# Extra identity products on TensorE before real work in a fused convolution, attention and expert kernel

## Chip, cores and metric

The kernel runs on one core of a Trainium2 chip. The metric is device time in microseconds (us), taken as the median of several runs. A profiled execution gives the time of every instruction; all durations below come from it. TensorE is written PE in profile lines (its weight loads PEld), VectorE DVE, ScalarE ACT, GpSimd POOL, and the engine that issues most DMAs SP (its queue SPq).

## What is computed

The reference has two layers on an image batch x of shape 2 x 256 x 56 x 56, all in fp32. Layer 0 normalises x by groups of 8 channels, makes queries, keys and values by a 1x1 convolution and a depthwise 3x3 one, runs neighbourhood attention (7x7 windows, half the heads with dilation 2), projects, and adds x. Layer 1 works on the 6272 pixels as tokens: linear attention with a feed-forward block, then a mixture of 8 experts of which each token uses two. Cut to its last lines:

```python
# --- layer 0 (conv_attn_hybrid) ---
x = x + _L0_conv_ref(_gn(x), L0_conv_w_qkv1, L0_conv_w_qkv2, L0_conv_rpb0, L0_conv_rpb1, L0_conv_w_proj)
# --- layer 1 (conv_attn_hybrid) ---
t = _to_tokens(x)
t = t + _L1_attn_ref(_ln_t(t), ...)   # elu(q)+1, elu(k)+1, sums over keys, W1, relu, W2
t = t + _L1_ffn_ref(_ln_t(t), ...)    # top 2 of 8 experts: gelu(x W1 + b1) W2 + b2, weighted
x = _from_tokens(t, x)
```

## The kernel before, in words

**Stages in order of time.** (1) Layer 0 of the first image, up to some 420 us: statistics on VectorE, group sums by two tiny products (gps, L478 and L484), the 1x1 convolution (py, L521), the depthwise one (a few rows as products pc, L542, the rest on VectorE as yc, L564 and L571), then attention: scores s_ps (L644), exp on ScalarE, bias on VectorE (p, L649), values po (L658), and the projection (L344, L349). The second image's convolutions fill gaps from here on. (2) Layer 1's attention for the first half of the tokens (the first image). `keys` runs over pairs of token tiles of 128: it transposes them (pts, L278), multiplies by the key weights (kps, L297) and adds to the key sums (kx, L309). `prepare_feed_forward` makes a bias (hb, L1788) while keys run. `queries`, `message` (pm, L1905), `feed_forward` (p, L1935; py, L1951) and `route` then run over groups of four tiles, staggered. (3) From 750 to 1045 us, attention of the second image, with the end of the first half's routing and the first expert tiles among it. `prepare` transposes queries and keys of four rows in four parts (`part`, into tiles x, L759); `rest` allocates one po tile for a half band, adds two chunks of values into it, and `done` has VectorE add it to acc (L832). GpSimd scatters tokens to the experts' rows (L167, xs); SP reads them back as xr (L1536) together with the expert's weights w1e, w2e and b2e. (4) Layer 1's attention for the second half, with expert tiles in between. (5) Expert tiles alone: ph (L1600), gelu, py (L1618), scatter-add to y (L167). Before and after the last ones `write` reads y back as yr, transposes it (pto, L2337) and stores it.

**What sets the order.** Each engine runs its instructions in program order. In stages 2 to 5 the order on TensorE is written out by hand (`tc.manual_schedule`, with strings such as "mqfkpPPPP" that name which step comes next). On the other engines and the DMA queues a scheduler sets it from its own estimate of when each instruction becomes ready, so a change on TensorE can move instructions elsewhere. An instruction that waits holds up all behind it on its engine.

**PSUM tiles.** Each product writes a PSUM tile from a pool. A tile's first write waits until the readers of the tile that was there before are done. The attention of one image has one po tile (`bufs=1`, two banks); the pool of x has two tiles; pts, kps, hb, pm, pto come from small pools of one bank a tile. A matmul with `start=True` overwrites what is there.

A product of fp32 operands shows as two MATMUL records in the profile.

Of the kernel before, what the change touches and what calls it, by code (L numbers as in the profile page):

```python
# [20 lines left out]
P = 128  # L21
B, C, HH, WW = 2, 256, 56, 56
# [6 lines left out]
NA = -(-T // 128)  # L29
# [16 lines left out]
E = 8  # L46
# [79 lines left out]
def hybrid_kernel(ctx: ExitStack, tc: tile.TileContext, a: dict, out: bass.AP):  # L126
    nc = tc.nc
# [3 lines left out]
    ident = const.tile([P, P], F32, name="ident")  # L131
# [33 lines left out]
    def scatter(dst, index, src, mine, others, **kw):  # L165
# [5 lines left out]
        apart(ins.ins, mine, others)  # L171
        return ins.ins

    evac_n = [0]

    newest = [None, None, None]
# [89 lines left out]
    def keys(tk, wk, sm, ps, bank, w_k, b2, kx, acc, n0, n, p, first, last, eager):  # L266


        t = tk.at(n0, n)[p]
        rows = p.stop - p.start  # L270
        mv, rs = stats(sm, t, tk.up[p, n0 : n0 + n], p)
        xt = wk.tile([P, 2, C + E], F32, name="xt", tag="u", bufs=3)[p, :, :C]
        pts = ps.tile([P, 2, 2 * P], F32, name="pts", tag="a")
        for k in range(n):
            with tc.high_priority() if eager else nullcontext():
                norm(xt[:, k, :], t[:, k, :], mv, rs, k)
            for ct in range(2):
                nc.tensor.transpose(  # L278
                    pts[:, ct, k * P : k * P + rows], xt[:, k, ct * P : (ct + 1) * P], ident[p, p]
                )  # L280
        xT = tk.turned(n0, n)[:, :, p] if n == 1 else tk.turned(n0, n)
        with tc.high_priority() if eager else nullcontext():
            evac(xT, pts[:, :, : n * rows])

        up = sm.tile([P, 2, 2], F32, name="up")[p]
        nc.vector.tensor_scalar(up[:, 0, :n], rs[:, :n], 1.0, None, ALU.add)
        nc.vector.scalar_tensor_tensor(up[:, 1, :n], mv[:, :n, 0], -1.0, rs[:, :n], ALU.mult, ALU.mult)
        for k in range(n):
            nc.scalar.activation(
                t[:, k, :], t[:, k, :], AF.Identity, bias=up[:, 1, k : k + 1], scale=up[:, 0, k : k + 1]  # L290
            )
        nc.gpsimd.tensor_tensor(t, t, b2[p].unsqueeze(1).to_broadcast([rows, n, C]), ALU.add)
        yield
        kps = bank()[p]
        for k in range(n):
            for ct in range(2):
                nc.tensor.matmul(  # L297
                    kps[:, k, :], xT[:, ct, k * rows : (k + 1) * rows], w_k[:, ct, :],
                    start=(ct == 0), stop=(ct == 1),
                )  # L300
        ks = wk.tile([P, 2, C], F32, name="ks", tag="mn")[p]
        elu1(
            wk, ks[:, :n, :].rearrange("p k c -> p (k c)"), kps[:, :n, :].rearrange("p k c -> p (k c)"),
            "k", 4, p,
        )
        yield
        for k in range(n):
            for hg in range(2):
                nc.tensor.matmul(  # L309
                    kx[:, hg, :], ks[:, k, hg * P : (hg + 1) * P], xt[:, k, :],  # L310
                    start=(first and k == 0 and hg == 0), stop=(last and k == n - 1), skip_group_check=True,
                )
        if first:
            nc.gpsimd.tensor_copy(acc, ks)
        else:
            nc.gpsimd.tensor_tensor(acc[p, :n, :], acc[p, :n, :], ks[:, :n, :], ALU.add)
        yield
# [93 lines left out]
    class Convolutions:  # L411
# [49 lines left out]
        def norm_image(self):  # L461


            sp, x_sb = self.sp, self.x_sb
            st = sp.tile([P, 2, NG, 6], F32, name="st")
            mv = sp.tile([P, 2, 2], F32, name="mv")
            for gs in (range(0, 3), range(3, NG)):
                for ct in range(2):
                    for g in gs:
                        nc.vector.bn_stats(st[:, ct, g, :], x_sb[:, ct, g * G : (g + 1) * G])  # L470
            for ct in range(2):
                anchors["stats"] = nc.vector.bn_aggr(
                    mv[:, ct, :], st[:, ct, :, :].rearrange("p g s -> p (g s)")
                ).ins
            yield
            gps = self.bank([P, 4], "gps")
            gm = sp.tile([P, 2], F32, name="gm")
            nc.tensor.matmul(gps[:, 0:2], self.g8, mv[:, :, 0], start=True, stop=True)  # L478
            nc.vector.tensor_copy(gm, gps[:, 0:2])
            dv = sp.tile([P, 2], F32, name="dv")  # L480
            nc.vector.tensor_tensor(dv, mv[:, :, 0], gm, ALU.subtract)
            nc.vector.tensor_tensor(dv, dv, dv, ALU.mult)
            nc.vector.tensor_tensor(dv, dv, mv[:, :, 1], ALU.add)
            nc.tensor.matmul(gps[:, 2:4], self.g8, dv, start=True, stop=True)  # L484
            with tc.high_priority():
                grs, anchors["pow"] = rstd_of(sp, gps[:, 2:4], 1e-5, "gn")
            yield
            for c0, c1 in zip((0, G, T // 2), (G, T // 2, T)):
                cols = slice(c0, c1)
                for ct in range(2):  # L490
                    nc.vector.tensor_scalar(
                        x_sb[:, ct, cols], x_sb[:, ct, cols],
                        gm[:, ct : ct + 1], grs[:, ct : ct + 1], ALU.subtract, ALU.mult,
                    )

        def run(self):
# [6 lines left out]
            for b, oc in ((b, oc) for b in range(B) for oc in range(6)):  # L503
                diag = None
                for hf in range(2):
# [10 lines left out]
                    ypad = self.ypads[hf]  # L516
                    q0 = r0 - hf
                    for g0, n in ((0, 8), (8, 8), (16, 8), (24, 5)):
                        py = self.bank([P, 8, WW], "py")
                        for ct in range(2):  # L520
                            nc.tensor.matmul(  # L521
                                py[:, :n, :], self.wq1[:, ct, oc * P : (oc + 1) * P],
                                self.x_sb[:, ct, (q0 + g0) * WW : (q0 + g0 + n) * WW],
                                start=(ct == 0), stop=(ct == 1),
                            )
                        k0 = 1 - hf + g0
                        anchors["copied"] = nc.scalar.copy(  # L527
                            ypad[:, k0 : k0 + n, 1 : WW + 1], py[:, :n, :]
                        ).ins
                        if not shared:  # L530
                            yield b, oc
# [67 lines left out]
    class Attention:  # L599
# [116 lines left out]
        def run(self):  # L716
# [72 lines left out]
            def prepare(g):  # L789
# [15 lines left out]

                def part(k):
                    pm = banks()
                    turned(lds, k, pm)
                    settle(g, k, pm)

# [32 lines left out]
            def band0(r):  # L843
# [22 lines left out]
                def chunk(hf, c):  # L866
# [10 lines left out]
                    def rest():  # L877
                        if c == 2 * hf:
                            po = self.ps_o.tile([P, 2, 512], F32, name="po")
                            sums[0] = po[:, :, : ni * 31].rearrange("p k (i j) -> p k i j", j=31)  # L880
                        h0 = (0, 25)[hf]
                        sub = sums[0][:, :, :, j0 - h0 : j1 - h0]
                        self.values(
                            TT, got[0], [(None, q, 0, v0[:, c, :], sub[:, 0], sub[:, 1])], c == 2 * hf
                        )
# [461 lines left out]
    class Experts:  # L1347
# [106 lines left out]

        def full_tiles(self, pc, ones):

            ce = self.counts(self.wp, pc, ones, self.tk.cnt, "ce1")
            nt = self.steps_below(self.wp, ce, 1, ALU.is_ge, "full")
            yield
            self.tab_a = yield from self.table(self.wp, "A", NTA, nt, self.ebase)  # L1460
# [179 lines left out]
    def linear(ph, tk, half, behind=None):  # L1640
# [140 lines left out]
        def prepare_feed_forward():  # L1781
            with tc.issue_after(newest[0]):
                centre(fw2[:, :, :C])

            hb_ps = ps_h.tile([P, 512], F32, name="hb", tag="h")
            for oc in range(4):
                for k in range(2):
                    nc.tensor.matmul(  # L1788
                        hb_ps[:, oc : oc + 1], fw1[:, 2 + k, oc * P : (oc + 1) * P], g1b1[:, k, 1:2],
                        start=(k == 0), stop=(k == 1),  # L1790
                    )
# [103 lines left out]
        def message(n0, n, qz, out):  # L1895
# [2 lines left out]
            ss = sm.tile([P, 4], F32, name="ssm")  # L1898
            for k0 in range(0, n, 2):
                pm = ps_h.tile([P, 2, C], F32, name="pm", tag="h")  # L1900
                for k in range(min(2, n - k0)):
                    for b, c0, c1 in parts(n0, n):
                        p, at = (slice(c0, c1), 0) if n == 1 else (slice(0, P), (k0 + k) * P)
# [260 lines left out]
    def layer1(whole, tk, conv_ctx=None, conv=None, behind=None):  # L2164
# [14 lines left out]
        with ExitStack() as ph:  # L2179
# [30 lines left out]
            def ending():  # L2210
# [4 lines left out]
                    pass  # L2215
                next(todo)
                yield
                table = ex.full_tiles(ln.bank()[:, :E], ln.ones)
                next(table)
                next(todo)  # L2220
                yield
# [78 lines left out]
        with ExitStack() as ph:  # L2300
# [28 lines left out]
                    apart(ins.ins, [f"yread{run}"], [f"yend{run}"], "tokens of early groups")  # L2329
                return n0, n, yr  # L2330

            def write(n0, n, yr, engines, places):
                for ct in range(2):
                    pool, tag = places[ct]
                    pt = pool.tile([P, 512], F32, name="pto", tag=tag)
                    for k in range(n):
                        nc.tensor.transpose(  # L2337
                            pt[:, k * P : (k + 1) * P], yr[:, k, ct * P : (ct + 1) * P], ident
                        )
# [39 lines left out]
                for _ in ex.run([(t, 2) for t in range(NFS, NTL)] + [(k, 1) for k in range(NHS, E)], pools):  # L2379
                    pass  # L2380
            last = [read(n0, n, False) for n0, n in order[early2:]]
            for h in held + last:
                write(*h, (nc.scalar, nc.sync), [(ps_t, "pt"), (ps_h, "ph")])

    with ExitStack() as ph:
        tokens = Tokens(ph, 0)
# [48 lines left out]
```

## Time and profile before

| what | us |
|---|---|
| median of 3 runs | 2003.97 |
| lowest and highest run | 2000.4, 2013.45 |
| profiled execution, its own time | 2003.56 |
| span of the profiled execution, first to last instruction | 2001.8 |
| TensorE busy in the span | 1842.0 |
| VectorE, ScalarE, GpSimd busy | 1094.2, 704.5, 582.2 |

A line of the timeline gives start, duration, engine, source line, output and inputs, shape, how many records it stands for, and in brackets the idle time of the engine before it and what ended it. A line of a table of stretches gives the stretch, its length, each engine's busy time with instruction counts, the granted TensorE clock (1 is full speed), the share of time that the DMA engines are busy, and GB/s. A line of the waits gives total, times and longest.

### The profile page before, as it was taken

Reading aid. Unit: us, or ns where it says so; the run is one execution under the profiler, and the core shown is the slowest. Engines: PE = TensorE matmul, PEld = TensorE weight load, DVE = VectorE, ACT = ScalarE, POOL = GpSimd, SP = SyncE. Lnnn points to the kernel's source line nnn. Section 1 sums busy time; section 2 is a strip of 40 time slices with the busy share of each in tenths; the row PEclk is TensorE's granted clock in tenths of the full one; section 3 lists DMA queues with packets and bytes.
Section 4 is the critical chain, followed back from the end, with each engine's and each line's share of the span. In section 5 each row is a group of like instructions: output and inputs, shape, how many; then the busy total and the mean of one; then the engine's idle time right before and its main releaser. Section 6 shows DMA issues by size and latency. Waiting matters only on the chain.

```text
span 2001.8 us, 27731 instructions
## 1 busy us (share of the span) xinstructions
PE 1842.0 (92%) x9996; PEld 1308.3 (65%) x9996; DVE 1094.2 (55%) x2733; ACT 704.5 (35%) x1331; POOL 582.2 (29%) x634
## 2 busy tenths in 40 slices
PE   6999898988889996899989989999899999999996
PEld 3545354556555654566668756567688888888885
DVE  6978988888887746555557434554531212121221
ACT  2333324324434323445536433323322232323332
POOL 4630221025102444111126311445422222222221
PEclk9999999989999996999999999999999999999998
DMA  4753432340001534654474211114577676766995
GB/s 112 160 138 110 133 92 75 111 146 17 25 38 42 157 85 145 193 152 134 129 201 127 56 34 37 48 57 132 156 230 200 188 199 189 198 190 195 299 279 161
DMA packets 200153, 268.85 MB, mean 134 GB/s; under 512 B 30953, under 2 KB 158615, under 8 KB 199761
## 3 DMA queue, kind: packets, MB, share of 16 engines
q1 hardware_dynamic: 167920, 223.95, 37.0%
q0 software_dynamic: 19728, 27.54, 7.5%
q10 hardware_dynamic: 12352, 15.43, 2.2%
q8 instruction: 83, 1.36, 0.3%
q14 instruction: 70, 0.57, 0.1%
HBM read 200.19 MB, written 70.95 MB: 135 GB/s over the span
## 4 chain that ended last, share of the span: by engine, by line
PE 47%; DMA 4%; DVE 4%; ACT 3%; issue 1%; POOL 1%; SPq 0%; ACTq 0%; DVEq 0%; POOLq 0%
PE ph L1600 13%; PE py L1618 13%; PE p L1935 4%; PE x L1618 2%; DMA y<-yt,idi 2%; PE x L1600 2%; PE py L1951 2%; PE po L658 2%; DMA xr<-xs 1%; PE kx L309 1%; PE kp L297 1%; PE x L349 1%; PE pm L1905 1%; PE s_ps L644 1%; PE px L1569 1%
## 5 line engine op out<-in xcount | busy, mean ns | idle before, releaser
L1600 PE MATMUL ph<-xe,w1e 128*128 128x256 f32 (+1 forms) x1448 | 312.1, 371 | 15.3 <-ACT hT L1604 9.4
L1618 PE MATMUL py<-w2e,hT 128*128 128x256 f32 x1392 | 311.5, 379 | 0.0
L1604 ACT ACTIVATE hT<-ph,sv 128x256 f32<-128x256 f32 (+1 forms) x362 | 165.7, 462 | 393.4 <-PE ph L1600 386.1
L1600 PEld LDWEIGHTS ph<-xe,w1e 128*128 128x128 f32 x1448 | 262.6, 191 | 55.0 <-ACT hT L1604 11.2
L1618 PEld LDWEIGHTS py<-w2e,hT 128*128 128x128 f32 x1392 | 260.2, 190 | 33.2 <-issue 0.2
L167 POOL DMA_INDIRECT y<-yt,idi x101 | 160.2, 1587 | 325.4 <-DVE yt L1624 186.9
L571 DVE SCALAR_TENSOR_TENSOR yc<-ypad,w,yc 128x1120 f32<-128x1120 f32 x144 | 202.8, 1412 | 26.4 <-ACT yc L561 18.5
L261 POOL TENSOR_TENSOR rs<-rs,mhalf 128x2 f32<-128x2 f32 (+3 forms) x90 | 72.1, 805 | 323.6 <-DVE rs L260 292.7
L521 PE MATMUL py<-x_sb,wq 128*128 128x448 f32 (+1 forms) x384 | 153.8, 532 | 5.4 <-ACT ypad L527 3.8
L648 ACT ACTIVATE p<-s_ps 112x952 f32<-112x952 f32 (+5 forms) x88 | 102.1, 1160 | 154.6 <-PE s_ps L644 96.0
L1552 DVE CAST idi<-xr 128x2 int32<-128x2 f32 (+1 forms) x53 | 9.8, 184 | 258.6 <-DMA xr<-xs 258.4
L649 DVE TENSOR_TENSOR p<-p,tab 112x952 f32<-112x952 f32 (+5 forms) x88 | 122.0, 1389 | 45.5 <-ACT p L648 39.6
L542 PE MATMUL pc<-ypad,diag 128*128 128x448 f32 x324 | 131.9, 548 | 0.0
L1624 DVE SCALAR_TENSOR_TENSOR yt<-py,eq,yt 128x256 f32<-128x256 f32 x87 | 41.8, 482 | 156.6 <-PE py L1618 156.4
L1582 POOL TENSOR_SCALAR yt<-b2e,eq 128x256 f32<-128x256 f32 x101 | 50.4, 505 | 251.5 <-DMA b2e<-in_L_ffn_b 209.0
L167 POOL DMA_INDIRECT xs<-row,si x98 | 100.5, 1026 | 71.9 <-DVE si L2082 41.9
L521 PEld LDWEIGHTS py<-x_sb,wq 128*128 128x128 f32 x384 | 71.7, 197 | 67.1 <-issue 56.8
L564 DVE SCALAR_TENSOR_TENSOR yc<-ypad,w,yc 128x784 f32<-128x784 f32 x96 | 101.8, 1077 | 4.2 <-ACT yc L561 3.6
L658 PE MATMUL po<-p,v 98*32 98x170 f32 (+5 forms) x960 | 71.2, 379 | 29.1 <-issue 12.6
L542 PEld LDWEIGHTS pc<-ypad,diag 128*128 128x128 f32 x324 | 59.8, 191 | 52.4 <-issue 48.7
L1935 PE MATMUL p<-m2T,fw 128*128 128x512 f32 (+2 forms) x224 | 93.8, 542 | 0.0
L1935 PE MATMUL p<-xT,fw 128*128 128x512 f32 (+1 forms) x208 | 92.7, 568 | 0.0
(391 smaller groups left out, 2891.1 us busy)
## 6 DMA issues: line engine op xcount, KB each, us to landing
w1e<-in_L_ffn_W SPq DMA_DIRECT2D x53, 1024.0 KB
w2e<-in_L_ffn_W SPq DMA_DIRECT2D x53, 1024.0 KB
yd<-yc SPq DMA_DIRECT2D x24, 784.0 KB
ld<-yd SPq DMA_DIRECT2D x28, 448.0 KB
xr<-xs SPq DMA_DIRECT2D x48, 260.0 KB
b2e<-in_L_ffn_b SPq DMA_DIRECT2D x53, 128.0 KB
t<-td SPq DMA_DIRECT2D x12, 512.0 KB
y<-t ACTq DMA_DIRECT2D x24, 256.0 KB
```

Of the source, the lines that this page charges most:

```text
L167: ins = nc.gpsimd.indirect_dma_start(out=dst[:, :], out_offset=bass.IndirectOffsetOnAxis(ap=index, axis=0), in_=src, in_offset=None, **kw,)
L521: nc.tensor.matmul(py[:, :n, :], self.wq1[:, ct, oc * P : (oc + 1) * P], self.x_sb[:, ct, (q0 + g0) * WW : (q0 + g0 + n) * WW], start=(ct ...
L542: nc.tensor.matmul(pc, diag[:, tap, :], ypad[:, dy : dy + SHARE, dx : dx + WW], start=(tap == 0), stop=(tap == 8),)
L564: nc.vector.scalar_tensor_tensor(yc[:, y0:y1, :], src, w, yc[:, y0:y1, :], ALU.mult, ALU.add)
L571: nc.vector.scalar_tensor_tensor(yc[:, y0:y1, :], src, w, yc[:, y0:y1, :], ALU.mult, ALU.add)
L648: nc.scalar.activation(p[:nk, :, :n], s_ps[:nk, :, :n], AF.Exp)
L649: nc.vector.tensor_tensor(grid(p), grid(p), table[:nk], ALU.mult)
L658: nc.tensor.matmul(dst[hs] if w is None else den[hs], v[:nk, hs] if w is None else w[:nk, :], p[:, h, :, o : o + q.shape[2]], start=first ...
L1600: nc.tensor.matmul(p1, x.w1[:, ct, j * P : (j + 1) * P], x.xe[:, ct, :], start=(ct == 0), stop=(ct == 1),)
L1604: nc.scalar.activation(hT[:, j, :], p1, AF.Gelu, bias=x.sv[:, 4 + j : 5 + j])
L1618: nc.tensor.matmul(py, hT[:, j, h * P : (h + 1) * P], x.w2[:, j, :], start=(j == 0), stop=(j == NJ - 1),)
L1935: nc.tensor.matmul(p1[:, :w], fw1[:, k, oc * P : (oc + 1) * P], rhs, start=(k == 0), stop=(k == 3))
```

## The change

A helper `hold(dst, n)` is new. It issues n products of the 128x128 identity by the identity repeated four times (128x512, fp32) into a PSUM tile that has just been allocated and that the real work then overwrites. It is called at ten call sites; where the number depends on the step, most steps get none. On the path that is executed 51 products are added: 11 before gps and 1 before the first py; 3, 1 and 2 before pts of token tiles 0, 10 and 20; 1 each before kps of tiles 0 and 27; 2 before hb of the first half; 2, 2 and 1 before pm of tiles 0, 4 and 29; 2 and 1 in the second image's transposes of parts 0 and 2 of the first rows; 4 in `full_tiles`; 4 each before po of two half bands of the second image (dilation 1, bands 1 and 2); 9 before the first pto behind the branch for further expert tiles. Three PSUM tiles are allocated wider, since a held product writes a whole bank. A branch that this input does not take holds the same again.

Nothing is removed, and the order on TensorE is otherwise the same (in the second image one run of 16 transposes is split in two by the products). The scheduler moves instructions on other engines: on VectorE mostly the convolution's yc against keys and routing, and one cast of idi ahead of four operations; on SP loads of ld, v, tab and x_s against xr, w1e and rb in the second image's attention.

```diff
+    def hold(dst, n):
+        for _ in range(n):
+            nc.tensor.matmul(
+                dst[:, : 4 * P], ident, ident.unsqueeze(1).to_broadcast([P, 4, P]),
+                start=True, stop=True, skip_group_check=True,
+            )
...
         pts = ps.tile([P, 2, 2 * P], F32, name="pts", tag="a")
+        hold(pts.rearrange("p ct t -> p (ct t)"), {0: 3, 10: 1, 20: 2}.get(n0, 0))
...
-        kps = bank()[p]
+        kps = bank()
+        hold(kps.rearrange("p k c -> p (k c)"), {0: 1, NA + 2: 1}.get(n0, 0))
+        kps = kps[p]
...
-            gps = self.bank([P, 4], "gps")
+            gps = self.bank([P, 512], "gps")
+            hold(gps, 0 if "copied" in anchors else 11)
...
-                        py = self.bank([P, 8, WW], "py")
+                        py = self.bank([P, 512], "py")
+                        hold(py, 0 if "copied" in anchors else 1)
+                        py = py[:, : 8 * WW].rearrange("p (r c) -> p r c", c=WW)
...
                     pm = banks()
+                    hold(pm, {(0, 0): 2, (0, 2): 1}.get((g, k), 0))
...
                             po = self.ps_o.tile([P, 2, 512], F32, name="po")
+                            hold(po[:, 0, :], {(1, 1, 0): 4, (1, 2, 0): 4}.get((b, r, hf), 0))
...
-            ce = self.counts(self.wp, pc, ones, self.tk.cnt, "ce1")
+            hold(pc, 4)
+            ce = self.counts(self.wp, pc[:, :E], ones, self.tk.cnt, "ce1")
...
             hb_ps = ps_h.tile([P, 512], F32, name="hb", tag="h")
+            hold(hb_ps, 0 if half else 2)
...
                 pm = ps_h.tile([P, 2, C], F32, name="pm", tag="h")
+                hold(pm.rearrange("p k c -> p (k c)"), {0: 2, 4: 2, NA + 4: 1}.get(n0 + k0, 0))
...
-            def write(n0, n, yr, engines, places):
+            def write(n0, n, yr, engines, places, warm=0):
...
                     pt = pool.tile([P, 512], F32, name="pto", tag=tag)
+                    hold(pt, warm * (ct == 0))
...
-                write(*h, (nc.scalar, nc.sync), [(ps_t, "pt"), (ps_h, "ph")])
+                write(*h, (nc.scalar, nc.sync), [(ps_t, "pt"), (ps_h, "ph")], 9 * (k == len(held)))
```

More of the change, by code (lines that the diff above doesn't have):

```diff
@@ L2217, in ending @@
                 yield
-                table = ex.full_tiles(ln.bank()[:, :E], ln.ones)
+                table = ex.full_tiles(ln.bank(), ln.ones)
                 next(table)
@@ L2381, in layer1 @@
             last = [read(n0, n, False) for n0, n in order[early2:]]
-            for h in held + last:
-                write(*h, (nc.scalar, nc.sync), [(ps_t, "pt"), (ps_h, "ph")])
+            for k, h in enumerate(held + last):
+                write(*h, (nc.scalar, nc.sync), [(ps_t, "pt"), (ps_h, "ph")], 9 * (k == len(held)))
     with ExitStack() as ph:
```

## The prediction

> **What bounds the kernel now.** I read the head of the page first (busy shares, the clock by slice), then the clock of the core, then TensorE's waits, then its timeline at the changed places, and last a table of short stretches with every engine's busy time.
>
> ```profile
> span 2001.8 us, 27731 instructions
> PE 1842.0 (92%) x9996; PEld 1308.3 (65%) x9996; DVE 1094.2 (55%) x2733; ACT 704.5 (35%) x1331; POOL 582.2 (29%) x634
> PE   6999898988889996899989989999899999999996
> PEclk9999999989999996999999999999999999999998
> core 0: 2001.8 us, clock 0.969
> ```
>
> TensorE bounds the whole: 92% busy. A mean clock of 0.969, when each dip is to 0.5, is (1 - 0.969) / 0.5 x 2001.8 = 124 us at half clock, worth at most 62 us. Slice 16 (750 to 800 us) holds the most.
>
> ```profile
> PE gps L478 <- DVE mv L472: 16.3, 2, 15.0
> PE pts L278 <- DVE xt L154: 13.3, 10, 4.1
> PE po L658 <- issue: 12.6, 6, 4.7
> PE pto L2337 <- DMA yr<-y: 11.1, 1, 11.1
> PE po L658 <- remote: 4.9, 1, 4.9
> ```
>
> These waits are where the products are put. The columns are total, times, longest.
>
> ```profile
> 554.31 0.75 PE L1905 MATMUL pm<-mw,qz 128*128 128x256 f32 x2 [3.14 <-DVE qz L1879]
> 556.45 5.84 PE L1905 MATMUL pm<-mw,qz 128*128 128x256 f32 x14 [1.39 <-DVE qz L1879]
> 563.64 3.60 PE L1865 MATMUL pq<-xT,w_q 128*128 128x512 f32 x8
> 789.88 1.02 PE L658 MATMUL po<-p,v 112*32 112x238 f32 x8 [4.87 <-remote]
> 837.20 1.02 PE L658 MATMUL po<-p,v 112*32 112x238 f32 x8 [4.67 <-issue]
> 1059.32 3.15 PE L297 MATMUL kp<-w_k,xT 128*128 128x256 f32 x8 [1.96 <-DVE xT L184]
> 1988.92 4.64 PE L2337 MATMUL pto<-ident,yr 128*128 128x128 f32 x26 [11.10 <-DMA yr<-y]
> ```
>
> After a wait the same work takes longer: eight kp records take 3.15 us at 1059.32 and 1.89 at 480.60. One fp32 product is two records (kps has four products, x8). From the pq row, 8 records by 3.43 us to the next start (567.07) give 0.86 us for a held product at full clock, so about 1.72 at half.
>
> ```profile
> 459.00:466.10 7.10, 6.26 (x14) 3.94 (x15) 7.10 (x13) 2.73 (x5) 4.50 (x5) 0.52 0.00 1
> 530.00:537.00 7.00, 5.52 (x18) 4.54 (x19) 7.00 (x12) 1.25 (x6) 0.00 (x0) 0.76 0.12 40
> 555.00:562.00 7.00, 5.61 (x15) 4.48 (x15) 5.80 (x8) 0.95 (x4) 1.32 (x1) 0.52 0.28 115
> 562.00:569.00 7.00, 7.00 (x19) 3.34 (x18) 5.55 (x8) 5.51 (x14) 1.49 (x2) 1.00 0.00 0
> 834.00:842.00 8.00, 4.80 (x32) 2.64 (x33) 5.90 (x13) 1.20 (x3) 0.01 (x1) 0.57 0.23 53
> 1060.00:1064.00 4.00, 4.00 (x15) 3.25 (x14) 2.24 (x3) 1.23 (x3) 1.59 (x1) 0.57 0.91 293
> ```
>
> Columns: length, busy PE, PEld, DVE, ACT, POOL, then clock. Here one sees whether a slow TensorE costs anything: in the first two rows VectorE is busy all the time, so a faster TensorE would only wait; in 1060 to 1064 TensorE is busy all the time and VectorE is not.
>
> **The change part by part.** Nothing is removed; 51 products are added, 44 us at full clock. Each can only start when its PSUM tile is free, and what it buys is clock.
>
> *What is at stake.* Ten stretches of the table lie behind changed places (424 to 432, 441 to 449, 459 to 466, 530 to 537, 555 to 562, 752 to 766, 773 to 784, 784 to 790, 834 to 842, 1060 to 1064). Length times (1 - clock), added up, is 33.8 us; TensorE is busy 77% of them, so 26 us could be won on TensorE, and only what TensorE bounds counts.
>
> *Start (gps 11, py 1).* Eleven products end before gps has its data at 14.95 (at half clock throughout, 11 x 1.72 = 19 would overrun by 5; with the clock up after some 4 us it is 13 to 14.5). py's 16 records at 18.58 take 7.41 us to the next start; four at 484.18 take 1.50, so 16 would take 6.0: 1.4 to be won. But between 15.5 and 18.58 TensorE has only two tiny products and one held one. Take 0.7, ends 0 and 1.4; work behind it is dense, so it carries.
>
> *First keys (pts 3, kps 1).* Both fit into waits of 4.06 and 1.33 us. They save about 2.8 us on kp and py, but TensorE then waits for g1b's load until 441.40 and VectorE for fw 6.2 us: 0, ends 0 and 0.5.
>
> *hb 2.* They follow kx without waiting, and run in the 2.55 us before g1b lands. The hb products themselves are 16 one-column records, so the clock may still fall; VectorE is busy 7.33 of the 8 us: 0.4, ends 0 and 1.6 (its 0.67 idle and the 0.97 it waits for elu_k).
>
> *pts 10 and 20, pm 0.* In waits of 2.00, 2.49 and 2.38 us. VectorE is busy 100% behind the first and third, and the clock is up behind the second. 0.2 together, ends -0.3 and 1.
>
> *pm 4.* Two products in the 3.14 us before 554.31. Fourteen pm records take 5.84 us; at 0.215 each (eight kp by 1.72) they would take 3.2. VectorE's 5.80 of 7 leaves room, and from 562 on TensorE is full. 2.4, ends 0 and 2.6.
>
> *part 2 and 1, full_tiles 4.* In the path of the transposes by 0.9 to 1.7 us each, but the stage 752 to 789 waits for POOL's scatters (16 at some 1.0 us busy and 0.3 of issue each, until 786.34, then the loads until 791.76). The half clock of 752 to 784 thus costs little and so do the products. 0.3, ends -1.5 and 3.
>
> *po (1,1,0) 4.* The tile is released by VectorE's acc, done at 789.77, and po ran at 789.88: four products stand in the way, at half clock until about 793.8, then at full, ending near 795.3. The po of 793.93 would start at 797.5: 3.6 late. Yet at 832.5 TensorE idles 4.67 us until data loaded over SP's queue (xr, issued 828.25, landed 835.17) arrive, which takes up the delay if that queue is not delayed too. -1.5, ends -5.4 and 0.
>
> *po (1,2,0) 4.* The tile is free at 836.04; po's data at 837.10. 3.44 us of products end at 839.5 at full clock, 2.3 after 837.2, and near 841 to 842 at half. Against it, 4.35 us of half-clock work (to 841.55) costs 2.2 too much now. -1.0, ends -5 and 1.
>
> *kps 27.* One product in 1.96 us of waiting. kp 3.15 to 1.89 and pts 1.06 to 0.60 are 1.7. TensorE is full behind. 1.5, ends 0 and 1.7.
>
> *pm 29.* After pd, before a qz that is late anyway (2.41 us): -0.3, ends -0.86 and 0.
>
> *pto 9.* 7.7 us in a wait of 11.1, over by 1986. The first 14 records of pto now take 2.93 us at half clock, the last 1.71 for as many: at most 1.2. The held work ends 3 us early, so the clock may be down again. 0.6, ends 0 and 1.2.
>
> *Order.* SP's loads of the second image move: between the xr loads issued at 810.82 and 828.25 there are 18 instead of 20 loads, 0.4 us of issue each, so the xr that TensorE waits for at 837.20 comes 0.8 us earlier, with w1e and rb four loads later. A cast idi on VectorE moves ahead of four operations that now hide in its 2.3 us wait. VectorE's yc move by one or two places in keys. 0.5, ends -2 and 2.
>
> Sum: 0.7 + 0 + 0.4 + 0.2 + 2.4 + 0.3 - 1.5 - 1.0 + 1.5 - 0.3 + 0.6 + 0.5 = 3.8 us gained. The profiled execution took 2003.56 (span 2001.8), 0.4 below the median of the runs, 2003.97; 2003.56 - 3.8 = 1999.8.
>
> **A rule against the trace.** In the 3.45 us from 1988.40 TensorE did only transposes (14 records, 2.93 us busy) at clock 0.50, and the next 3.40 us ran at 1.00: here transposes bring the clock back. The Trainium skill, "TensorE: Matmul & The Clock Gate", Part 4: PE-mode transpose, says that they do not count as busy in the same way. By that rule the transposes of 752 to 766 could not restore the clock but the held products could, and the part term would go to its upper end, 3 instead of 0.3, and the time to 1997.1; the row decides. The same page, Part 1, What's actually happening, puts the ramp at under 1% of a typical span, which speaks against a large gain: as an estimate, under 20 us here. The trace has 124 us at half clock, more than that rule expects.
>
> **The rivals.** *A: the clock is worth more than the waits suggest.* If the engines' slack absorbs little, the 26 us and the ends of start (1.4) and pto (1.2) come in full: 28.6, less 4 for the products in the path: 1979. At two thirds it is 1988. Speaks for it: 92% busy. Against it: VectorE's 100% in two stretches, POOL in the largest. It needs about 20 us to be 1% faster.
>
> *B: held products delay the real work.* At the two po spots eight products start only when the tile is free, just when the real data come. If they run at half clock and SP's wait does not take the delay up, that is 5.4 + 5 = 10.4 instead of 2.5, and 1999.8 + 7.9 = 2007.7; it makes the kernel slower from 6.3 us on. With the lower end of the order, 2 instead of -0.5, 2010.2. For over 1% some 12 held products at 1.72 would have to stand in the path.
>
> *C: no clock is won.* If one or two products are too little for the clock, the pm 4, kps 27, start and pto terms (5.2) vanish: 2005.0.
>
> **How the numbers follow.** My forecast has 0.58, A 0.24, B 0.10, C 0.08. The range goes to half-way between A's full price and two thirds (1984), and on the other side to B with the lower end of the order (2010.2) and some 2 us of the spread of the runs: 1984 to 2012. The likeliest case alone reaches from 1992 to 2006. About 1%, 20 us, is what a measurement of this kernel can tell from no change. Faster by over 1% is most of A, 0.18; slower a part of B, 0.05; the rest, 0.77, is within 1%.
>
> **What would show it.** The mean clock should rise from 0.969 to about 0.98; kp after the 1.96 us wait should fall to 1.9 us and the pm of 556 to some 3.2; pts and pm 0 should show a higher clock and longer waits instead of an earlier end. po after the hold should start 3.6 us later behind acc, and the 4.67 us wait shrink. The forecast is wrong if VectorE's stretches shorten with the clock (A), if the time from 790 to 845 grows by more than 4 us (B), or if the clock after the holds stays at 0.5 (C).

## The result

In 22 runs of each kernel on one chip the changed kernel took 2000.13 us (median) and the kernel before 2005.97. The ratio (changed to before, here and below) is 0.9968, with a 95% interval of 0.9958 to 0.9978: about 6.4 us faster, 4.4 to 8.4 by the interval, inside 1%. The forecast was 3.8 us. The profiled execution of the changed kernel took 2001.02 us (span 1999.2), 0.9 above its median, and that of before 2003.56, 2.4 below the median of its 22 runs, so the two profiles show only 2.5 of the 6.4 us between them.

The head of the page of the changed kernel, and the clock of its core:

```profile
span 1999.2 us, 27936 instructions
PE 1877.4 (94%) x10098; PEld 1317.6 (66%) x10098; DVE 1094.6 (55%) x2733; ACT 703.8 (35%) x1331; POOL 585.3 (29%) x634
PEclk9999899999999997999999999999999999999999
core 0: 1999.2 us, clock 0.978
```

TensorE is busier by 35 us (102 more records) and the mean clock rises from 0.969 to 0.978, that is from 124 to (1 - 0.978) / 0.5 x 1999.2 = 88 us at half clock. Those 36 us are worth at most 18. The span shrinks by 2.6 us, the runs by 6.4: most of what the clock gives is not time.

TensorE's waits in the changed kernel (total, times, longest; L177 is the held product):

```profile
PE pts L287 <- DVE xt L154: 4.1, 7, 1.1
PE po L177 <- remote: 2.1, 1, 2.1
PE gps L490 <- DVE mv L483: 1.7, 2, 0.9
PE pto L2357 <- DMA yr<-y: 1.7, 2, 1.3
```

The long waits of gps (15.0), pto (11.1) and po (4.7 and 4.9) are gone as waits, because the held products fill them. That alone says nothing about time.

The timeline of the changed kernel at the same places as before:

```profile
546.86 0.70 PE L1924 MATMUL pm<-mw,qz 128*128 128x256 f32 x2 [1.41 <-DVE qz L1897]
549.00 4.97 PE L1924 MATMUL pm<-mw,qz 128*128 128x256 f32 x14 [1.44 <-DVE qz L1897]
555.32 3.60 PE L1883 MATMUL pq<-xT,w_q 128*128 128x512 f32 x8
781.43 5.37 PE L177 MATMUL po<-ident 128*128 128x512 f32 x8 [2.11 <-remote]
786.72 0.61 PE L672 MATMUL po<-p,v 112*32 112x238 f32 x8
833.58 3.61 PE L177 MATMUL po<-ident 128*128 128x512 f32 x8
837.12 0.61 PE L672 MATMUL po<-p,v 112*32 112x238 f32 x8
1058.14 1.99 PE L308 MATMUL kp<-w_k,xT 128*128 128x256 f32 x8 [1.09 <-DVE xT L192]
1977.24 7.96 PE L177 MATMUL pto<-ident 128*128 128x512 f32 x18 [1.49 <-DVEq L2398]
1986.50 1.09 PE L2357 MATMUL pto<-ident,yr 128*128 128x128 f32 x8 [1.29 <-DMA yr<-y]
1988.03 2.41 PE L2357 MATMUL pto<-ident,yr 128*128 128x128 f32 x18 [0.44 <-DMA yr<-y]
```

kp after its wait takes 1.99 instead of 3.15 us (one profile of each; the table below has all), po 0.61 instead of 1.02, pto's 26 records 1.09 and 2.41 instead of 4.64. The 14 pm records of 549 take 4.97 instead of 5.84, not the 3.2 that were forecast. Held products cost what was worked out: eight records take 3.61 us at full clock and 5.37 where half of them run at half clock.

The stretches of the changed kernel behind pm 4, around po (1,2,0) and around kps 27 (length, busy PE, PEld, DVE, ACT, POOL, clock):

```profile
546.50:553.50 7.00, 5.19 (x15) 3.98 (x16) 6.10 (x9) 0.95 (x4) 0.56 (x1) 0.76 0.14 57
834.00:842.00 8.00, 8.00 (x56) 4.21 (x58) 5.53 (x11) 2.64 (x6) 0.00 (x0) 1.00 0.34 96
1057.00:1061.00 4.00, 2.90 (x16) 2.55 (x16) 3.93 (x6) 0.82 (x2) 2.24 (x2) 1.00 0.75 133
```

The clock is 1.00 in two of them, and 0.76 behind pm 4.

### The profile page after: what moved, and what is told of

It is laid out like the page before. It is cut to its first block, busy times and chain, and to the rows that moved or that the text cites. A ratio compares the mean times of both kernels' runs of the same rounds, so it can differ in the third digit from the quotient of the medians.

```text
span 1999.2 us, 27936 instructions
## 1 busy us (share of the span) xinstructions
PE 1877.4 (94%) x10098; PEld 1317.6 (66%) x10098; DVE 1094.6 (55%) x2733; ACT 703.8 (35%) x1331; POOL 585.3 (29%) x634
## 4 chain that ended last, share of the span: by engine, by line
PE 49%; DMA 4%; DVE 3%; ACT 3%; issue 1%; POOL 1%; SPq 0%; ACTq 0%; DVEq 0%; POOLq 0%
PE py L1635 13%; PE ph L1617 13%; PE p L1954 4%; PE x L1635 2%; DMA y<-yt,idi 2%; PE x L1617 2%; PE py L1970 2%; PE po L672 2%; DMA xr<-xs 2%; PE pm L1924 1%; PE kx L320 1%; PE kp L308 1%; PE x L360 1%; PE pq L1883 1%; PE px L1586 1%; PE s_ps L658 1%
## 5 line engine op out<-in xcount | busy, mean ns | idle before, releaser
L1970 PE MATMUL py<-fw,hTl 128*128 128x264 f32 x392 | 91.6, 390 | 0.8 <-issue 0.5
```

Source lines behind the costliest of these rows:

```text
L1970: nc.tensor.matmul(py[:, : C + E], hT[:, kk, c0 : c0 + P], fw2[:, kk, :], start=(kk == 0), stop=(kk == 3),)
```

## The experiments

Twelve further measurements were made on three chips, each beside the kernel before on the same chip. The kernel before differs between chips (medians 1996.29, 2007.41 and 2006.41), so only ratios on one chip are compared. All edits are to the changed kernel; a place that is switched off keeps its line, with 0 products. Each edit is shown cut to some of its lines, and the sentence beside it says which sites keep their products.

**First chip: which part wins, which loses?** Lining up the starts of the same records in the profiles of before and after, the changed kernel was 7.3 us ahead at 740 us and 0.8 behind at 800. My theory from this: the early groups win, and the products in the second image's attention give it back. The first test leaves out the second image's products alone (`part`, po and `full_tiles`):

```diff
-                    hold(pm, {(0, 0): 2, (0, 2): 1}.get((g, k), 0))
+                    hold(pm, 0)
...
-                            hold(po[:, 0, :], {(1, 1, 0): 4, (1, 2, 0): 4}.get((b, r, hf), 0))
+                            hold(po, 0)
...
-            hold(pc, 4)
+            hold(pc, 0)
```

> All held products but those in the second image's attention (part, full_tiles, po: 15 of the 51 left out). Theory: by the starts of the same records in the two profiles the change is 7.4 us ahead at 745 us and level at 800; the products of the second image stand in the path (counts, then scatters; then po) and give the gain back. Without them the time should be 3 to 8 us below the full change, a ratio to before of 0.993 to 0.9955, and the lead at 800 us should stay at 6 or more. Rival: the stage from 750 to 840 us is set by scatters and xr loads and swallows any lead; then the ratio is that of the full change, 0.996 to 0.998, and the lead at 840 is 2 us again.

Measured: 0.9973 (0.9957 to 0.9988). Above the theory's 0.993 to 0.9955, where the rival put it.

The opposite: `hold` with 0 products at gps, py, pts, kps, hb, pm of `message` and pto; only the three sites above keep theirs.

```diff
-        hold(pts.rearrange("p ct t -> p (ct t)"), {0: 3, 10: 1, 20: 2}.get(n0, 0))
+        hold(pts, 0)
...
-            hold(hb_ps, 0 if half else 2)
+            hold(hb_ps, 0)
...
-                    hold(pt, warm * (ct == 0))
+                    hold(pt, 0)
```

> Only the 15 held products of the second image's attention. Theory: they cost what the full change loses between 745 and 800 us, less the absorption by the xr wait: 3 to 7 us slower than before, ratio 1.0015 to 1.0035. Rival (the stage swallows the lead whatever is held): within 1.5 us of before, 0.9993 to 1.0007; the forecast's own terms (0.3 - 1.5 - 1.0 and 0.5 for SP's order) give 1.7 us slower, 1.0008.

Measured: 1.0045 (1.0029 to 1.0061), 9 us slower, above what either expected. Alone they cost; together with the others they don't show. The two results don't fit a plain sum, since 0.9973 and 1.0045 would make 1.0018. The profiled execution of this kernel, 1998.02 us, was the fastest of its 7 runs (median 2003.8), so its trace does not hold the 9 us.

Only the first keys and hb (pts 0, kps 0, hb):

```diff
-        hold(pts.rearrange("p ct t -> p (ct t)"), {0: 3, 10: 1, 20: 2}.get(n0, 0))
+        hold(pts.rearrange("p ct t -> p (ct t)"), {0: 3}.get(n0, 0))
...
-        hold(kps.rearrange("p k c -> p (k c)"), {0: 1, NA + 2: 1}.get(n0, 0))
+        hold(kps.rearrange("p k c -> p (k c)"), {0: 1}.get(n0, 0))
...
+                            hold(po, 0)
+            hold(pc, 0)
+                    hold(pt, 0)
```

(gps, py, part and pm are off as well.)

> Only 6 of the 51: 3 before pts of tile 0, 1 before kps of tile 0, 2 before hb of the first half. Theory: TensorE's faster first keys let SP's queue issue g1b earlier and keep the clock up, some 5.5 us at 448 us in the profile, most of which carries until 745: 3 to 6 us faster, ratio 0.997 to 0.9985. Rival (the forecast: waits for g1b and a busy VectorE take it back): 0 to 1 us, 0.9995 to 1.0.

Measured: 1.0008 (0.9997 to 1.0018). The theory falls, the forecast's term (0 for pts and kps, 0.4 for hb) stands.

All but `full_tiles`:

```diff
-            hold(pc, 4)
+            hold(pc, 0)
```

> The full change without the 4 products of full_tiles. Theory: they end at 771.9 us, the count product behind them waits, and with it the second batch of scatters: 2 to 4 us faster than the full change, ratio 0.9945 to 0.996. Rival: the count was late anyway and the products only raise the clock: as the full change, 0.9965 to 0.9975, or slower than it.

Measured: 0.9972 (0.9957 to 0.9988), where the rival put it; the full change, measured on another chip, had 0.9968. This speaks against a count that delays the scatters, though the interval still touches what that theory expected (up to 0.996).

**Second chip: the other groups one by one.** Only gps and py keep products:

```diff
             gps = self.bank([P, 512], "gps")
             hold(gps, 0 if "copied" in anchors else 11)
...
                         hold(py, 0 if "copied" in anchors else 1)
```

> Only the 12 products at the start (gps 11, py 1); the order on the other engines is that of before. The forecast's term: 0.7 us won, ends 0 and 1.4, ratio 0.9993 to 1.0. Theory after the first profile of the full change (py reads x_sb 0.75 us earlier there, but runs at half clock until 23.7 us, and is 0.3 us late at 30): nothing, 0.9995 to 1.0005.

Measured: 0.999 (0.9974 to 1.0007): not told apart from nothing nor from the forecast's 0.7 us. Its profile shows where the forecast erred. First this kernel, then a second profile of the kernel before, from the same chip:

```profile
14.66 0.38 PE L490 MATMUL gps<-mv,g 128*128 128x2 f32 x2 [0.94 <-DVE mv L483]
15.88 0.38 PE L496 MATMUL gps<-dv,g 128*128 128x2 f32 x2
17.88 8.57 PE L535 MATMUL py<-x_sb,wq 128*128 128x448 f32 x16 [1.62 <-DVE x_sb L503]
```

```profile
14.90 0.58 PE L478 MATMUL gps<-mv,g 128*128 128x2 f32 x2 [14.90 <-DVE mv L472]
16.32 0.59 PE L484 MATMUL gps<-dv,g 128*128 128x2 f32 x2 [0.84 <-DVE dv L483]
18.53 8.58 PE L521 MATMUL py<-x_sb,wq 128*128 128x448 f32 x16 [1.61 <-DVE x_sb L491]
```

py is no faster (8.57 and 8.58). What the products buy is 0.2 us on each of the two tiny products ahead of it. py starts 0.65 us earlier, but 0.24 of that was there at the first tiny product (14.66 against 14.90), which waits for VectorE's mv. Why py is no faster shows in the clock (stretch, length, busy PE, clock, DMA share, GB/s): it has fallen again by the time that py runs.

```profile
16.90:23.60 6.70, 5.72 (x8) 0.50 0.81 33
```

Only pts 10 and 20 and pm 0 and 4:

```diff
+        hold(pts.rearrange("p ct t -> p (ct t)"), {10: 1, 20: 2}.get(n0, 0))
...
+                hold(pm.rearrange("p k c -> p (k c)"), {0: 2, 4: 2}.get(n0 + k0, 0))
```

> Only pts of tiles 10 and 20 (1 and 2 products) and pm of tiles 0 and 4 (2 each). The forecast's terms: 2.6 us won, nearly all at pm 4, ratio 0.9985 to 0.999. Theory of groups that don't add up (first_keys alone brought nothing, the second image alone cost 9 us, all together won 6): the starts at 570 to 740 us are 2 to 3 us ahead, and a part of it is lost by 840: 0.9985 to 1.0. Rival: the whole gain of the change is here, 4 to 7 us, ratio 0.9965 to 0.998.

Measured: 0.9982 (0.9966 to 0.9998), 3.6 us. Its timeline, then that of the second profile of before:

```profile
528.39 1.96 PE L177 MATMUL pm<-ident 128*128 128x512 f32 x4
530.92 3.72 PE L1924 MATMUL pm<-mw,qz 128*128 128x256 f32 x16 [0.56 <-DVE mw L1752]
548.83 1.88 PE L177 MATMUL pm<-ident 128*128 128x512 f32 x4
554.26 3.29 PE L1924 MATMUL pm<-mw,qz 128*128 128x256 f32 x14 [1.44 <-DVE qz L1897]
```

```profile
531.17 6.24 PE L1905 MATMUL pm<-mw,qz 128*128 128x256 f32 x16 [2.38 <-DVE mw L1735]
556.14 5.29 PE L1905 MATMUL pm<-mw,qz 128*128 128x256 f32 x14 [0.92 <-DVE qz L1879]
```

The starts of later records show both gains as time: against the second profile of before this kernel is 0.3 us ahead at 531, 1.9 at 546, 3.9 at 562, 3.2 at 740. So 1.6 us are gained around pm 0, which the forecast had at about nothing, and 2.0 around pm 4.

Only kps 27, pm 29 and pto:

```diff
+        hold(kps.rearrange("p k c -> p (k c)"), {NA + 2: 1}.get(n0, 0))
...
+                hold(pm.rearrange("p k c -> p (k c)"), {NA + 4: 1}.get(n0 + k0, 0))
```

> Only kps 27 (1 product), pm 29 (1) and pto (9). The forecast's terms: 1.5 - 0.3 + 0.6 = 1.8 us won, ratio 0.999, ends 0.9985 and 1.0. By the profile of the full change kps 27 gives 1.7 and pto 0.8: 0.9985 to 0.999. Rival: a gain of 4 or more, 0.998 or less, since this stage is the one that TensorE bounds without a break.

Measured: 0.9985 (0.9967 to 1.0003), 3.0 us with an interval that holds the forecast's 1.8 and nothing.

The last one on this chip is the kernel before, without an edit.

> The kernel before, unchanged, for a second profile of it beside those of the experiments. All theories expect its time within 5 us of the other runs of it on the same chip; the starts of its records against the first profile show how far two profiles of one kernel lie apart at 740, 840 and 1400 us, which says what differences of starts mean anything: under 2 us if the differences of chips lie in few places.

Measured: 2008.30 us. Against the first profile of the same kernel its records start 2.0 us later at 400, level at 740, 4.7 us later at 845, 6.3 at 1040 and 4.6 at 1990. My expectation of under 2 us was wrong: the starts of two single profiles say nothing about differences of a few us over a long way. My theory on the first chip had been read from just that.

**Third chip: the full change beside its parts.** Two kernels were run again without a new edit: the full change, and the one without the second image's products.

> The full change again, now beside the others of this call on one chip. Theory 1 (the groups add up, chips apart: start -2.0, first keys +1.6, mid -3.6, late -3.0, second image +9): about level with before, 0.999 to 1.0025. Theory 2 (the second image's products cost only what a TensorE that comes late there cannot hide; with the lead of the other groups they cost nothing): 0.996 to 0.998, as at first.

Measured: 0.9969 (0.9955 to 0.9982).

> All but the second image's 15 products, again, beside the full change on one chip. Theory 1: 9 us below the full change, a ratio lower by 0.0045. Theory 2: within 2 us of the full change, ratios within 0.001 of each other. Both expect 0.9955 to 0.998 against before.

Measured: 0.9969 (0.9956 to 0.9983), level with the full change. Here the second image's products neither cost nor gain; the interval of each reaches some 2.7 us either way. The two profiles, from one chip, show what happens, place by place. SP's xr loads and the VectorE operation that waits for the second of them, with the products off:

```profile
804.58 0.37 SPq L1553 DMA_DIRECT2D xr<-xs  x1
823.84 0.35 SPq L1553 DMA_DIRECT2D xr<-xs  x1
830.61 0.17 DVE L1569 CAST idi<-xr 128x2 int32<-128x2 f32 x1 [10.16 <-DMA xr<-xs]
831.40 1.14 DVE L663 TENSOR_TENSOR p<-p,tab 112x952 f32<-112x952 f32 x1
832.64 1.02 PE L672 MATMUL po<-p,v 112*32 112x238 f32 x8 [6.89 <-issue]
```

With them:

```profile
744.70 3.19 PE L177 MATMUL x<-ident 128*128 128x512 f32 x4 [3.60 <-DVE prob L2021]
804.83 0.37 SPq L1553 DMA_DIRECT2D xr<-xs  x1
821.08 0.35 SPq L1553 DMA_DIRECT2D xr<-xs  x1
827.00 0.17 DVE L1569 CAST idi<-xr 128x2 int32<-128x2 f32 x1 [2.84 <-DMA xr<-xs]
829.29 3.61 PE L177 MATMUL po<-ident 128*128 128x512 f32 x8
```

Starts of the full change against no_second: 3.9 us late at 744 (the two products of part (0,0) stand in the path of the transposes), 1.5 ahead at 784, 3.7 late at 801 (po (1,1,0)), 2.4 ahead at 838. The last step is 6.1 us in its favour: without the products TensorE idles 6.89 us (po needs p, which stands on VectorE behind the cast that waits for xr), which takes up the 3.7; with them xr is issued 16.3 us after the one before instead of 19.3, and po behind it runs at full clock. The order on SP between the two is the scheduler's new one, with a load of tab in place of one of v; the number of loads between is 20 in both. The pair is an extreme one: over all fourteen profiles the distance is 16.3 to 17.2 us (mean 16.7) in the five with the po products, and 17.0 to 19.6 (mean 18.3) in the nine without.

Only the po products:

```diff
                             hold(po[:, 0, :], {(1, 1, 0): 4, (1, 2, 0): 4}.get((b, r, hf), 0))
```

> Only the 8 products before po (1,1,0) and (1,2,0), which alone move SP's loads; VectorE's order is that of before but for one cast. The forecast's terms: -1.5 - 1.0 + 0.5, 2.0 us slower, ratio 1.001, ends 1.005 and 0.9995. Theory 1, if it is these that cost the 9 us: 1.003 to 1.005. If it is part and full_tiles (counts and scatters late): 0.9995 to 1.001.

Measured: 0.9997 (0.9978 to 1.0015): the forecast's 2.0 us of cost lies inside, and so does a gain.

The groups that measured below before, together:

```diff
+        hold(pts.rearrange("p ct t -> p (ct t)"), {10: 1, 20: 2}.get(n0, 0))
+        hold(kps.rearrange("p k c -> p (k c)"), {NA + 2: 1}.get(n0, 0))
...
+            hold(hb_ps, 0)
+                    hold(pm, 0)
+                            hold(po, 0)
+            hold(pc, 0)
```

(The pm line is that of `part`; `message`, gps, py and pto keep theirs.)

> The three groups that each measured below before: start (12), pts of tiles 10 and 20 and pm of tiles 0 and 4 (7), kps 27, pm 29 and pto (11). Where their gains add up: 8.6 us faster, ratio 0.9957, ends 0.9945 and 0.997, so 2 us below the full change. Rival: they overlap with what the first keys win, and the ratio is that of no_second, 0.997.

Measured: 0.9955 (0.9938 to 0.9973), where the sum of the groups put it. With 30 of the 51 products it is the lowest ratio of all, but its interval overlaps that of the full change (0.9955 to 0.9982), so it isn't shown to be better. Against no_second it leaves out the first keys only. Its waits from 420 to 570 us, then those of no_second on the same chip:

```profile
PE pts L287 <- DVE xt L154: 11.5, 8, 4.3
PE hb L1806 <- DMA g1b<-in_L_attn_b: 1.4, 1, 1.4
```

```profile
PE pts L287 <- DVE xt L154: 4.8, 7, 1.1
PE kp L308 <- DVE xT L192: 2.8, 2, 2.5
PE pts L177 <- DVE t_i L192: 2.5, 1, 2.5
```

With the first keys' products the long wait for xt is filled, others for VectorE's xT and t_i appear, and the starts of the two kernels lie 0.2 us apart at 500 us.

**One table over all profiles.** Fourteen executions were profiled: of before (two), of the full change (two) and of the partial kernels (ten). The duration of the same records, by whether held products stood ahead of them:

| records | without held products | with |
|---|---|---|
| py, first 16 | 7.11 to 8.58, mean 7.92 (7 profiles) | 7.14 to 8.77, mean 7.90 (7) |
| pm 0, 16 | 5.12 to 6.25, mean 5.68 (7) | 3.72 in each (7) |
| pm 4, 14 behind the wait | 5.28 to 6.26, mean 5.76 (7) | 3.29 (4), 4.97 to 4.98 (3) |
| po (1,2,0), 16 | 1.81 to 1.82 (9) | 1.01 (5) |
| kp of tile 27, 8 | 1.99 (3), 2.61 to 3.18 (4), mean 2.53 | 1.99 in each (7) |
| from the last py to the end | 23.52 to 24.25, mean 23.94 (7) | 22.67 to 23.57, mean 23.06 (7) |

Whether a faster record is time shows in the distance between the starts of two records, one ahead of the place and one behind it (named by their starts in the first profile of before; all profiles have the same order on TensorE there):

| from, to | without held products | with |
|---|---|---|
| first instruction to py 18.58 | 18.38 to 18.63, mean 18.48 (7) | 17.83 to 18.77, mean 18.06 (7) |
| pm 531.48 to py 546.85 (pm 0) | 15.35 to 16.09, mean 15.55 (7) | 13.74 to 13.75 (7) |
| py 541.38 to pq 563.64 (pm 4) | 20.57 to 23.37, mean 22.08 (7) | 18.48 to 18.49 (4), 20.17 (3) |
| x 784.40 to x 826.30 (po (1,1,0)) | 41.31 to 45.61, mean 43.72 (9) | 45.57 to 48.81, mean 46.79 (5) |
| x 826.30 to x 850.60 (po (1,2,0)) | 22.97 to 27.28, mean 24.81 (9) | 21.07 to 22.68, mean 21.39 (5) |
| py 1055.47 to px 1099.10 (kps 27) | 41.96 to 44.05, mean 43.01 (7) | 41.93 to 42.36, mean 42.00 (7) |

At pm 4 and kps 27 the clock itself is time. The two groups of pm 4 with products, whose VectorE order there is the same, lie 1.69 us apart in both tables (3.29 and 4.98, 18.48 and 20.17). At kps 27 the three profiles without a product whose kp took 1.99 needed 41.96 to 42.25 us, the four with a slower kp 43.61 to 44.05. For the full change the differences of the means (pm 4 by its 20.17) and the end make 0.4 + 1.8 + 1.9 - 3.1 + 3.4 + 1.0 + 0.9 = 6.3 us, where the runs show 6.4. That they meet so closely is luck: the ranges are wide, and the first keys, pts 10 and 20, `part`, `full_tiles` and pm 29 are not in the sum.

## Why the prediction was right, point by point

The sign and the case (the forecast's own, inside 1%) were right. The size came out too small: 3.8 us lies below the interval of 4.4 to 8.4 of the first measurement, and just inside that of the third chip (3.6 to 9.0). The mechanism was right in parts. Of the terms:

- **Start, 0.7.** 0.4 us by the means of the table. The mechanism was another: py is not faster, as the clock has fallen again when it runs; the two tiny products are.
- **First keys and hb, 0.4.** 1.0008 alone (0.9997 to 1.0018) fits it. That the waits of VectorE and the loads took the gain back fits the waits above, but was not tried by itself.
- **pts 10, pts 20, pm 0: 0.2.** This is the gain that was missed: 1.8 us around pm 0 alone. The forecast read that VectorE is busy all of 530 to 537 us, so that a faster TensorE would only wait. For the order that VectorE had, this holds: in five of the seven profiles without products pm 0 took anything from 5.12 to 6.25 us, and py 546.85 started 15.35 or 15.36 us behind pm's start in all five. What failed is that the forecast took this order as fixed (its order term has yc moving only in keys). First VectorE in the kernel before, then in the one with pts 10, pts 20, pm 0 and pm 4 alone:

```profile
531.42 5.76 DVE L564 SCALAR_TENSOR_TENSOR yc<-ypad,w,yc 128x784 f32<-128x784 f32 x6
537.09 0.17 DVE L260 TENSOR_SCALAR rs<-ssm 128x2 f32<-128x2 f32 x1
540.03 0.17 DVE L260 TENSOR_SCALAR rs<-ssm 128x2 f32<-128x2 f32 x1 [0.89 <-ACT sq L1799]
```

```profile
530.86 2.91 DVE L578 SCALAR_TENSOR_TENSOR yc<-ypad,w,yc 128x784 f32<-128x784 f32 x3
533.96 0.17 DVE L268 TENSOR_SCALAR rs<-ssm 128x2 f32<-128x2 f32 x1 [0.19 <-ACT sq L1817]
```

  yc is the second image's convolution, which the scheduler fills into gaps; rs is what the stage needs from pm. Six yc stand ahead of the first rs in all seven profiles without products, three in all seven with them, and rs starts 3.04 instead of 5.61 us behind pm's start. No run has the new order without the products, so the shares of order and clock are not separated here. As an estimate, with a slow pm the order alone would bring rs 0.8 us forward: in the second profile of before the sq that rs reads ended at 535.97, and rs ran at 536.79.
- **pm 4, 2.4.** 2.0 in the pair of profiles, 1.9 in the full change by the table, since there the clock falls in 546.5 to 553.5 us after all (0.76, 4.97 us).
- **kps 27, 1.5.** Mis-sized: I took the 3.15 us of one profile as what always happens. Over seven profiles without the product the mean is 2.53, 0.54 above that with it, and with the work behind it 1.0 us is gained.
- **pto, 0.6.** 0.9 by the last line of the first table.
- **pm 29, -0.3.** Not tried alone.
- **part and full_tiles, 0.3.** full_tiles: nothing measured (0.9972 without, 0.9968 with, on different chips). part stands in the path for 3.9 us at 744 in the pair of profiles, more than the 1.7 I had for its two products; there it is taken up later.
- **po, -2.5, and the order on SP, +0.5.** -2.0 together, measured 0.6 us faster (4.4 faster to 3.0 slower), so the forecast lies inside too. By the table the first po loses 3.1 us, near the 3.6 that I expected, and the second wins 3.4, where I had a loss. There po runs in 1.01 instead of 1.82 us, and xr is issued earlier by 1.6 us on the mean instead of the 0.8 that I had worked out from 18 loads instead of 20: the trace has 20 in both orders.

Rival A asked for 16 to 25 us: the clock gained 36 us of half-clock time, worth at most 18, but 6.4 came out. Rival B (products in the path) fits what only_second shows, 9 us slower, if none of the other groups is there, but that its cause is B is not shown; beside the other groups it does not appear. Rival C is excluded for pm, po, kp and pto by the tables, and holds for py.

The rule weighed against a row was not tried by an edit, but the row repeats: in each of the seven profiles without the products of pto, the 3.41 us step at half clock just ahead of the return to full clock holds nothing but pto's transposes, with TensorE busy 0.86 to 1.00 of it. The comparison there of 124 us with 20 set a time at half clock beside a loss; the loss is at most 62.

**What stays open.** Why the second image's 15 products cost 9 us alone on one chip (7 runs) while the full change and the kernel without them are level on another. po alone costs nothing there, so part and full_tiles with a TensorE that has no lead are what is left, or the chip; neither was tried by itself. How much of pm 0's gain the new order on VectorE would bring without the products is open, and whether the first keys' products should go (0.9955 against 0.9969) isn't settled either.

## What to carry to other kernels

Filling a wait with dummy products can buy clock, but count it only where the slow records feed the chain. Where another engine is busy all the time, look what with: filler work there does bind as long as it stands ahead of what the chain needs, and ceases to when the scheduler moves it behind. A dummy product that can start only when its tile is free belongs ahead of a long wait that ends for another reason, and a change on one engine can win more through the order it gives a DMA queue than through what it does. Judge effects of 0.3% by many runs on one chip, and local effects by the duration of the same records, and the distance between two of them, over several profiles, not by the starts in one pair.

## What the runs showed of the hardware

Within one execution the stretches at half clock begin on a fixed grid of 3.413 us and, but for the one that the end of the trace cuts off, last whole steps of it, in all fourteen profiles. In the last profile of the full change all 14 begin at 1.177 to 1.180 modulo 3.4133. The grid lies elsewhere in each execution (0.42 in the second profile of before, 2.27 in no_second's second). So the same kernel, with the same waits, has a stretch at half clock in one execution and not in another. In the first profile of before kp after its 1.96 us wait took 3.15; in the second:

```profile
1065.58 1.99 PE L297 MATMUL kp<-w_k,xT 128*128 128x256 f32 x8 [1.96 <-DVE xT L184]
```

That fits the Trainium skill, "TensorE: Matmul & The Clock Gate", Part 1, What's actually happening: a window of 3413 ns that runs free of the kernel's start.

The grid also explains why pm 4's 14 records took 3.29 us in four profiles with products and 4.98 in three. Cut along the grid, the wait ahead of them falls into one step of the full change, and into two of the kernel with pts 10, pts 20, pm 0 and pm 4 alone (step, length, busy PE, clock, DMA share, GB/s):

```profile
545.94:549.35 3.41, 1.04 (x4) 1.00 0.00 0
```

```profile
549.05:552.47 3.42, 2.01 (x6) 1.00 0.00 0
552.47:555.88 3.41, 1.97 (x10) 1.00 0.00 0
```

In the three slow profiles one step is busy for 0.24 to 0.42 of its length and the next runs at half clock; in the four fast ones no step there is below 0.51. Over all fourteen profiles, of the steps at full clock that were busy for less than 0.40, all 123 were followed by half clock; of those between 0.40 and 0.60, 83 of 196; above 0.60, 23 of 7354. From half clock the return came only behind steps that were busy for 0.84 or more (216 times). These shares rest on ends of products that the profile models.

The clock in the profile reads 1.00 until its first change, but TensorE can be slow there: in the first profile of before that change is at 22.35 us, and py's records start 0.75 us apart ahead of it and 0.38 behind it. The mean clocks, and the 124 and 88 us, leave that first stretch out.
